# Twenty-four early gathers of a graph attention layer, put by in DRAM, and scores as columns of the first product

## The chip, the core and the metric

The kernel runs on one core of a Trainium2 chip. A core has TensorE (PE in the profile; its weight loads are listed apart as PEld), VectorE (DVE), ScalarE (ACT), GpSimd (POOL) and SyncE (SP, which here only issues DMAs), an on-chip memory of 128 partitions (SBUF), the accumulators of TensorE (PSUM), and 16 DMA engines to and from the chip's DRAM. Each engine runs its own instructions in order, and the engines wait for one another by semaphores. The metric is the time of one execution in microseconds on the device, the median of several runs.

## The reference

A layer norm (no scale or shift) and a ReLU, then a graph network with two attention layers (GAT), a two-layer perceptron, and the sum with the input. There are 6,250 nodes, 100,000 edges and one loop per node; inputs are float32, and the edges are sorted by destination.

```python
def gat_conv(x, src, dst, W, a_src, a_dst, bias, heads):
    h = (x @ W).reshape(n, heads, -1)
    alpha_s = (h * a_src[None]).sum(-1)
    alpha_d = (h * a_dst[None]).sum(-1)
    e = leaky_relu(alpha_s[src] + alpha_d[dst], 0.2)
    m = segment_max(e, dst);  e = exp(e - m[dst])
    alpha = e / (segment_sum(e, dst)[dst] + 1e-16)
    return segment_sum(h[src] * alpha[:, :, None], dst).reshape(n, -1) + bias

h = relu(layernorm(x))                     # 6250 x 768
h = relu(gat_conv(h, ..., W1, heads=4))    # 4 heads of 64
h = relu(gat_conv(h, ..., W2, heads=1))    # 1 head of 256
out = x + relu(h @ Wm1 + bm1) @ Wm2 + bm2
```

## The kernel before

The nodes are cut into NT = 49 tiles of 128, the edges into 782 tiles of 128 in their sorted order. Four edge tiles make a group (NG = 196 groups), four groups belong to a node tile.

**Stage 1** (lines 305 to 463) runs over the 49 node tiles. DVE takes means and variances (`moments`, L320 to L322) and subtracts the mean (`centre`, L339), ACT applies the ReLU (L341), and TensorE multiplies with W1 in six steps of K = 128 (`features1`, L350). A float32 product stands in the profile as two records, so a tile has twelve. ACT scales the result into a row tile `kept[i]` (`keep1`, L356). POOL multiplies it with the eight score vectors a_src, a_dst and adds it in halves (L365, L368); for the last four tiles DVE does this product (L375). DVE sums the rest (`scores1`, L377), ACT appends the four source scores to the row (L378), and `store1` (L381, SP) writes the row tile to `table[1]` in DRAM: 264 float32 per node, four heads of 64 and a one each, then four scores. `edge_places` loads and prepares the edge lists in small pieces, one per tile from tile 14 on; `first_places` (L278, at tile 40) makes the index lists of the early gathers.

**Layer 1** (`layer_edges` with `Node1`) and **layer 2** (`Node2`) then run over the 196 groups. `gather` (L545) has POOL fetch, for each edge tile, the 128 source rows out of `table` by one indirect DMA (L554), eight groups ahead of their use. Two edge tiles share a buffer; there are 2 * (AHEAD + 2) = 20 such pair buffers (L225). `meet` (L600) brings the destination's score to each edge by a product with a mask, `pair` (L612) makes the attention weights (ACT L619 and L621, DVE L624 and L634) and the weighted rows `hw` (DVE L636 in layer 1), and TensorE adds them up per destination with the one-hot matrix `hot` (DVE L582) into `o_ps` (L648). `gather_up` adds partial sums of groups, and `node.steps` (L796) finishes a node tile: it divides, turns it (two transposes into the PSUM tile `tp`), multiplies with the second layer's weights and writes the row to `table[2]` (L819). The steps are spread over the following groups by `rest(7)`: each `advance` (two per group) lets each pending node tile do one step, and near the end `rest` gives way at once. The PSUM tiles `tp` and `h_ps` take turns in two buffers (tag "n").

**Early gathers.** A gather from the whole table has to wait for the last row tile. `EARLY` lists gathers that read only the first `there` row tiles: sources beyond them are replaced by row 0 (`first_i`), multiplied with 0 (`first_ok`), and the missing rows added by a product of a one-hot matrix (`first_hits`, L258) with the row tiles that are still in SBUF (`first_whole`, L273 and L275). In layer 1 there are eight: four with `there` = NT - 5 and four with NT - 3, issued by POOL in stage 1's tiles NT - 4 and NT - 2 (`first_rows`, L300). Layer 2 has eleven.

The order on each engine is the program's order (`tc.manual_schedule()`, L304); a tile's buffer comes free when all its users are done. SP issues, in this order, what the loops ask for: x tiles, row stores, the destination rows `drow` (L521, three buffers), the masks (L573, kept in DRAM for layer 2), the rows of table 2.

Of the kernel before, what the change touches and what calls it, by code (L numbers as in the profile page):

```python
# [17 lines left out]
P = 128  # L18
# [28 lines left out]

EARLY = {1: ((4, NT - 5), (4, NT - 3)), 2: ((2, NT - 3), (9, NT - 2))}
THERE = {layer: [there for n, there in stages for _ in range(n)] for layer, stages in EARLY.items()}

@with_exitstack
def kernel(
# [52 lines left out]

    iota_ps = ps.tile([P, P], F32, name="iota_ps", bufs=1)
    nc.vector.tensor_copy(iota_ps, iota)
    eps_c = const.tile([P, 1], F32, name="eps_c")  # L110
    nc.vector.memset(eps_c, EPS)
# [77 lines left out]
    def edge_places(ones):  # L189

        dst_i = ones.tile([P, NET], I32, name="dst_i")
        dri = ones.tile([NCH, CH], I32, name="dri")
        for to, of in ((dst_i, dst_cols), (dri, dst_rows), (src_i, src_cols)):
            nc.sync.dma_start(to, of)
            yield
            yield
        for layer in bT:
# [64 lines left out]
    def first_whole(pool, layer):  # L262

        j = 0
        for stage, (n, there) in enumerate(EARLY[layer]):
            if stage and layer == 1:
                first_hits(pool, layer, stage)
            for k in range(n):
                pair, t = divmod(FIRST + j, 2)
                G = first_G[layer][pair][:, t]  # L270
                p = ps.tile([P, TW[layer]], F32, name="missing", tag="o", bufs=3)
                for T in range(there, NT):
                    nc.tensor.matmul(p, hits[stage, T][:, k * P:(k + 1) * P], kept[T][:, :TW[layer]],  # L273
                                     start=(T == there), stop=(T == NT - 1))
                nc.vector.scalar_tensor_tensor(G, G, first_ok[layer][:, j:j + 1], p, ALU.mult, ALU.add)  # L275
                j += 1
# [15 lines left out]
    def first_rows(layer, stage):  # L292
# [3 lines left out]
        for j in range(j, j + n):  # L296
            k, t = divmod(FIRST + j, 2)
            if k not in first_G[layer]:
                first_G[layer][k] = rows_in(layer)
            nc.gpsimd.indirect_dma_start(  # L300
                out=first_G[layer][k][:, t], out_offset=None, in_=table[layer][:there * P],
                in_offset=bass.IndirectOffsetOnAxis(ap=first_i[layer][:, j:j + 1], axis=0))
    mask_d = dram.tile([NU * P, 8 * P], BF16, name="mask_d")
    edges_stack.enter_context(tc.manual_schedule())  # L304
    with tc.tile_pool(name="w1p", bufs=1) as wp, tc.tile_pool(name="x1", bufs=6) as xp, \
# [38 lines left out]
        def features1(i):  # L344
            r, rstd = rs.pop(i)
            h_ps = ps.tile([P, HID], F32, name="h_ps", tag="o", bufs=3)
            for k in range(KI):
                if (i, k) == (1, 2):
                    spread_means(2)
                nc.tensor.matmul(h_ps, r[:, k], w1[:, k], start=(k == 0), stop=(k == KI - 1))  # L350
            return h_ps, rstd

        def keep1(i, h_ps, rstd):
            row = kept[i]
            h = heads_row(row)[:, :, :HID // 4]
            nc.scalar.activation(h, h_ps.rearrange("p (h c) -> p h c", h=4), AF.Copy, scale=rstd)  # L356

            ha = wk.tile([P, 8, HID // 4], F32, name="ha", bufs=2)
            four = ha.rearrange("p (k h) c -> p k h c", k=2)
            of = h.unsqueeze(1).to_broadcast([P, 2, 4, HID // 4])  # L360
            if i >= NT - 4:
                halves[i] = four, of
                return
            else:
                nc.gpsimd.tensor_tensor(four, of, a1b, ALU.mult)  # L365
                for n in (HID // 8, HID // 16):
                    hb = wk.tile([P, 8, n], F32, name=f"ha{n}", bufs=2 if n > 16 else 4)
                    nc.gpsimd.tensor_tensor(hb, ha[:, :, :n], ha[:, :, n:], ALU.add)  # L368
                    ha = hb
            halves[i] = ha  # L370

        def scores1(i):
            if i >= NT - 4:
                four, of = halves[i]
                nc.vector.tensor_tensor(four, of, a1b, ALU.mult)  # L375
                halves[i] = four.rearrange("p k h c -> p (k h) c")
            nc.vector.tensor_reduce(sd[1][:, i], halves.pop(i), AX.X, ALU.add)  # L377
# [18 lines left out]
        fetch_x(1)  # L396
        w1 = wp.tile([P, KI, HID], F32, name="w1")
        nc.sync.dma_start(w1, W1.rearrange("(k p) f -> p k f", p=P))
        fetch_xT(1)
# [5 lines left out]
        fetch_x(5)  # L405
        pieces = edge_places(ones)
        moments(0)
        spread_means(0)
# [5 lines left out]
        for i in range(NT):  # L414
# [23 lines left out]
            if i == 40:  # L438
                first_places()
            if i < NT - 5:  # L440
                keep1(i, *h)
                if i > 2:
                    store1(i - 3)
                if i > 1:
                    scores1(i - 2)
            else:
                for k in {NT - 3: (i - 2, i - 1)}.get(i, (i - 2,) if i < NT - 3 else (i - 1,)):
                    scores1(k)
                    if k == NT - 7:
                        store1(k - 1)  # L450
                    store1(k)
                keep1(i, *h)
            if i == NT - 6:
                first_sources(1)
            if i == NT - 4:
                first_rows(1, 0)
            elif i == NT - 2:
                first_rows(1, 1)
            if i >= 14:
                next(pieces, None)  # L460

        scores1(NT - 1)
        store1(NT - 1)

# [65 lines left out]
    def layer_edges(layer, H, node, pre, matched, pre_pool):  # L530
# [4 lines left out]
        with tc.tile_pool(name=f"eg{layer}", bufs=5) as eg, \  # L535
# [9 lines left out]
            def gather(g):  # L545
                if not 0 <= g < NG:
                    return
                for t in tiles(g):
                    k = TPG * g + t
                    if k // 2 not in G:  # L550
                        G[k // 2] = first_G[layer].get(k // 2) or rows_in(layer)
                    if k < FIRST + len(THERE[layer]):
                        continue
# [140 lines left out]
            if layer == 1:  # L694
                for r in range(4):
                    fetch_rows(r)
                first_whole(pre_pool, layer)
                for u in range(4):
# [9 lines left out]
            for g in range(NG):  # L708
# [14 lines left out]
                if j == 0:  # L723
                    if layer == 1:
                        fetch_rows(t + 4)
                    node.prefetch(t)
                    meet(t + 1)
                elif j == (2 if t < NT - 1 else 1):
                    node.ahead(t)
                elif j % 2:  # L730
                    make_mask((g + 7) // 2)
                if g == NG - 3:
# [40 lines left out]
    with tc.tile_pool(name="w2p", bufs=1) as wp, tc.tile_pool(name="wk2", bufs=2) as wk:  # L773
# [4 lines left out]
        class Node1:  # L778
# [17 lines left out]
            def steps(self, t, sum_, most=None, last=None):  # L796
# [12 lines left out]
                turn(o, p)  # L809
                yield from rest(7)  # L810
                rT = straighten(wk, 1, p)
                h_ps = ps.tile([P, HID + 2], F32, name="h_ps", tag="n")
                for k in range(KH):
                    nc.tensor.matmul(h_ps, rT[:, k], w2[:, k], start=(k == 0), stop=(k == KH - 1))
                yield from rest(7)
                row = kept[t][:, :TW[2]]
# [5 lines left out]
        with tc.tile_pool(name="pre1", bufs=1) as pre:  # L822
            first_hits(pre, 1, 0)
            pre1 = prepare(pre, 1, 4)
# [430 lines left out]
```

## Time and profile before

| | us |
|---|---|
| median of 3 runs | 2144.38 (2143.71 to 2145.70) |
| profiled execution | 2556.39 |
| its span, first to last instruction | 2554.4 |

The profiled execution is longer than the runs that were timed without the profiler, and every trace time below is on its clock.

| engine | busy us | share of the span | instructions |
|---|---|---|---|
| PE | 1572.4 | 62% | 6764 |
| DVE | 1325.8 | 52% | 4164 |
| ACT | 545.2 | 21% | 2601 |
| POOL | 1599.2 | 63% | 1759 |

Stage 1 takes the first 155 us, layer 1's edges reach to about 1355 us, layer 2's to the end. A group of the profile is read as: line, engine and operation, output <- inputs, shapes and count, then busy time in us and the mean of one in ns, then the idle time of its engine just before, with what ended most of it. Two rows as an example: the first product of stage 1, and the early completions' products.

```profile
L350 PE MATMUL h_ps<-w,r 128*128 128x256 f32 x588 | 135.0, 384 | 4.4 <-ACT r L341 4.4
L300 POOL DMA_INDIRECT G<-table,first_i x19 | 19.2, 1011 | 46.8 <-DVE e_ps L634 40.0 <-issue 4.9 <-DMA table<-kept 1.7
```

The records of L350 overlap: 588 of them have a mean of 384 ns, but only 135.0 us are busy. The L300 row is POOL's early gathers of both layers, 1.01 us each.

### The profile page before, as it was taken

The numbers are of one execution on the slowest core, as the hardware profiler recorded it, in microseconds if no ns is written. First come the engines' busy times: TensorE is split into PE (matmuls) and PEld (weight loads), VectorE is DVE, ScalarE is ACT, GpSimd is POOL, SyncE is SP. The second block draws the span as 40 slices with busy tenths as digits, with TensorE's granted clock in tenths as the row PEclk, the third lists the DMA queues.
The fourth block names the chain that finished last, engine by engine and source line by source line (L and its number), as shares of the span: only waits on it lengthen the run. The fifth ranks groups of instructions, "written<-read, shape, count | busy, mean of one in ns | idle before, by whom it ended". The sixth has DMA issues, their size and how long they took to land.

```text
span 2554.4 us, 26518 instructions
## 1 busy us (share of the span) xinstructions
PE 1572.4 (62%) x6764; PEld 1116.8 (44%) x6765; DVE 1325.8 (52%) x4164; ACT 545.2 (21%) x2601; POOL 1599.2 (63%) x1759
## 2 busy tenths in 40 slices
PE   9963455545554556546554557666676676666667
PEld 7852334433433334324342444444454444444444
DVE  7844555555655556546562444444444444444444
ACT  4630111111121111112121112222222222222212
POOL 6875666666666666666635566666666666666661
PEclk9986677667777777777776777777877787778789
DMA  9954454445454454444434444544554455445442
GB/s 353 344 164 145 128 148 138 132 138 150 135 147 140 136 149 141 137 136 146 138 91 134 125 134 130 152 149 136 155 151 144 142 153 152 144 144 153 147 150 66
DMA packets 157543, 383.12 MB, mean 150 GB/s; under 512 B 35543, under 2 KB 50222, under 8 KB 157382
## 3 DMA queue, kind: packets, MB, share of 16 engines
q0 software_dynamic: 75072, 209.10, 30.4%
q1 hardware_dynamic: 80940, 170.75, 19.1%
q10 hardware_dynamic: 1370, 1.48, 0.2%
q8 instruction: 58, 0.95, 0.1%
q14 instruction: 103, 0.84, 0.1%
HBM read 323.07 MB, written 58.13 MB: 149 GB/s over the span
## 4 chain that ended last, share of the span: by engine, by line
DVE 18%; another core or an unknown queue 15%; PE 14%; issue 13%; ACT 3%; DMA 0%; POOL 0%; ACTq 0%; DVEq 0%; POOLq 0%
PE o_ps L648 8%; DVE hw L631 6%; DVE hw L636 3%; PE y_ps L939 3%; DVE e_ps L624 2%; DVE w L627 1%; PE tp L923 1%; ACT sum L678 1%; DVE acc L669 1%; DVE y L942 1%; DVE e_ps L634 1%; PE e_ps L600 1%; DVE hot L582 1%; PE y_ps L875 0%
## 5 line engine op out<-in xcount | busy, mean ns | idle before, releaser
L554 POOL DMA_INDIRECT G<-table,src_i x1545 | 1469.0, 951 | 822.9 <-issue 535.8
L648 PE MATMUL o_ps<-hw,hot 128*128 128x260 f32 x1564 | 541.4, 482 | 316.2 <-issue 204.4
L648 PEld LDWEIGHTS o_ps<-hw,hot 128*128 128x128 f32 x1564 | 344.8, 235 | 482.5 <-issue 278.6
L648 PE MATMUL o_ps<-G,hw 128*128 128x258 f32 x1564 | 488.2, 460 | 61.3 <-issue 41.2
L648 PEld LDWEIGHTS o_ps<-G,hw 128*128 128x128 f32 x1564 | 352.8, 233 | 168.7 <-issue 59.6
L624 DVE TENSOR_TENSOR e_ps<-e,e_ps 128x8 f32<-128x8 f32 (+1 forms) x782 | 126.5, 162 | 515.7 <-ACT e L621 172.4
L678 ACT ACTIVATE sum<-acc 32x260 f32<-32x260 f32 (+1 forms) x384 | 159.9, 416 | 991.4 <-DVE acc L669 730.4
L600 PE MATMUL e_ps<-win,mask 128*128 128x12 bf16 (+1 forms) x1564 | 88.2, 169 | 372.7 <-issue 356.5
L636 DVE TENSOR_TENSOR hw<-G,e_ps 128x520 f32<-128x520 f32 x391 | 271.9, 695 | 76.9 <-DVE e_ps L634 46.3
L631 DVE TENSOR_SCALAR hw<-iota_ps,dcol,w 128x128 f32<-128x128 f32 x782 | 285.0, 406 | 17.7 <-DVE w L627 2.9
L600 PEld LDWEIGHTS <-mask 128*128 128x128 bf16 x1564 | 75.2, 103 | 393.5 <-issue 369.3
L942 DVE TENSOR_TENSOR y<-y_ps,xt 128x384 f32<-128x384 f32 (+1 forms) x98 | 54.0, 552 | 233.5 <-remote 209.6
L619 ACT ACTIVATE e<-G 128x8 f32<-128x8 f32 (+1 forms) x782 | 151.4, 195 | 110.5 <-issue 57.7
L939 PE MATMUL y_ps<-wm,mT 128*128 128x384 f32 x392 | 160.9, 535 | 11.1 <-issue 7.5
L582 DVE TENSOR_TENSOR hot<-iota_ps,dcol 128x512 f32<-128x512 f32 x196 | 133.5, 681 | 34.1 <-remote 34.1
L621 ACT ACTIVATE e<-G 128x8 f32<-128x8 f32 (+1 forms) x782 | 149.4, 192 | 0.0
L350 PE MATMUL h_ps<-w,r 128*128 128x256 f32 x588 | 135.0, 384 | 4.4 <-ACT r L341 4.4
L923 PE MATMUL tp<-rT,wm 128*128 128x128 f32 x392 | 68.0, 328 | 111.4 <-issue 81.9
L634 DVE TENSOR_TENSOR e_ps<-e_ps,e 128x8 f32<-128x8 f32 x391 | 68.1, 174 | 131.5 <-remote 96.4
L769 ACT ACTIVATE rT<-tp,bT 128x128 f32<-128x128 f32 x196 | 60.7, 362 | 293.5 <-remote 243.3
L350 PEld LDWEIGHTS h_ps<-w,r 128*128 128x128 f32 x588 | 109.7, 193 | 22.6 <-ACT r L341 5.7
L923 PEld LDWEIGHTS tp<-rT,wm 128*128 128x128 f32 x392 | 59.8, 229 | 125.6 <-issue 91.1
(405 smaller groups left out, 1201.3 us busy)
## 6 DMA issues: line engine op xcount, KB each, us to landing
xt<-in_x SPq DMA_DIRECT2D x96, 384.0 KB
drow<-dmod_d SPq DMA_DIRECT2D x49, 512.0 KB
mask_d<-mask SPq DMA_DIRECT2D x97, 256.0 KB
mask<-mask_d SPq DMA_DIRECT2D x97, 256.0 KB
G<-table,src_i POOLq DMA_INDIRECT x1545
xTt<-in_xT SPq DMA_DIRECT2D x49, 384.0 KB
out<-y SPq DMA_DIRECT2D x48, 384.0 KB
table<-kept SPq DMA_DIRECT2D x49, 132.0 KB
```

Of the source, the lines that this page charges most:

```text
L350: nc.tensor.matmul(h_ps, r[:, k], w1[:, k], start=(k == 0), stop=(k == KI - 1))
L554: nc.gpsimd.indirect_dma_start(out=G[k // 2][:, k % 2], out_offset=None, in_=table[layer], in_offset=bass.IndirectOffsetOnAxis(ap=src_i[:, ...
L582: nc.vector.tensor_tensor(hot[g][:, T[0]:T[0] + n], iota_ps.unsqueeze(1).to_broadcast([P, n, P]), dcol[:, k:k + n].unsqueeze(2).to_broadca ...
L600: nc.tensor.matmul(e_ps[t][:, at + k, :3 * H], m[:, k * P:(k + 1) * P], pre.win[:, 2 * u + 2], start=True, stop=True)
L619: nc.scalar.activation(e1, sc, AF.Exp)
L624: nc.vector.tensor_mul(v, e2, rho)
L631: nc.vector.tensor_scalar(hw[:, t], iota_ps, dcol[:, k:k + 1], w[:, t], ALU.is_equal, ALU.mult)
L636: nc.vector.tensor_mul(hw, Gp[:, :, :RW[1]].rearrange("p t (h c) -> p t h c", h=H), w.unsqueeze(3).to_broadcast([P, 2, H, C + 1]))
L648: nc.tensor.matmul(o_ps[u], l, r[:, :RW[layer]], start=(g % 2 == 0 and k == 0), stop=(g % 2 == 1 and k == tiles(g)[-1]))
L678: nc.scalar.activation(done[t][r], acc[r], AF.Copy)
L923: nc.tensor.matmul(m_ps[:, j], wm1[:, k, j * P:(j + 1) * P], rT[:, k], start=(k == 0), stop=(k == KH - 1))
L939: nc.tensor.matmul(y_ps, mT[:, j], wm2[:, j, s * half:(s + 1) * half], start=False, stop=(j == KH - 1))
```

## The change

**Early gathers of layer 1.** `EARLY[1]` goes. In its place twelve pairs of edge tiles (24 gathers) are listed in `SOON` by the number of row tiles that their gathers may read (NT - 11 to NT - 2); they belong to the pairs 23, 39, 55, ... 199, one in every eight groups (`SOON_AT`). In stage 1, from tile 35 on, each row tile is stored at once, and `soon_rows` issues the gathers that this row tile allows. When the edges begin, `soon_away` writes the twelve pair buffers to DRAM; `soon_back` reads one back where the loop before would have gathered it. `soon_sources`, `soon_hits`, `soon_missing` and `soon_whole` complete one edge tile per node tile for the first 24 node tiles: SP loads the source numbers, DVE makes the one-hot matrices in group 2 of the node tile, TensorE multiplies them with the row tiles in group 3 (into a PSUM tile of tag "n"), and DVE adds the product to the row in the next node tile's group 1. `rest(7)` becomes `rest(4)` in layer 1's steps.

**Scores.** W1 gets eight more columns, W1 times the score vectors, computed by POOL and DVE (`halve` and a reduce at tiles 2 to 4). From tile 8 (`BARE`) on the product has 264 columns, and ACT copies the scores from PSUM to the row and to `sd`. The first eight tiles still use POOL, at tiles 4 to 11, and DVE, at tiles 8 to 15. The index lists of the 24 gathers are made among the pieces of `edge_places`.

```diff
-EARLY = {1: ((4, NT - 5), (4, NT - 3)), 2: ((2, NT - 3), (9, NT - 2))}
+EARLY = {2: ((2, NT - 3), (9, NT - 2))}
+SOON = [NT - m for m in (11, 11, 10, 9, 8, 7, 6, 5, 4, 4, 3, 2)]
+SOON_AT = {2 * (8 * i + 11) + 1: i for i in range(len(SOON))}
+BARE = 8
...
+    def soon_places(i):
+        of = src_i[:, 2 * soon_pair[i]:2 * soon_pair[i] + 2]
+        nc.vector.tensor_scalar(soon_ok[:, i], of, float(SOON[i] * P), None, ALU.is_lt)
+        nc.vector.tensor_tensor(soon_i[:, i], of, soon_ok[:, i], ALU.mult)
+    def soon_rows(there):
+        for i in range(len(SOON)):
+            if SOON[i] == there:
+                soon_G[i] = rows_in(1)
+                for t in range(2):
+                    nc.gpsimd.indirect_dma_start(
+                        out=soon_G[i][:, t], out_offset=None, in_=table[1][:there * P],
+                        in_offset=bass.IndirectOffsetOnAxis(ap=soon_i[:, i, t:t + 1], axis=0))
+    def soon_away():
+        for i in range(len(SOON)):
+            nc.sync.dma_start(soon_d[i], soon_G.pop(i).rearrange("p t c -> p (t c)"))
+    def soon_back(i):
+        G = rows_in(1)
+        nc.sync.dma_start(G.rearrange("p t c -> p (t c)"), soon_d[i])
+        return G
+    def soon_sources(pool, i):
+        if i < len(SOON):
+            soon_of[i] = pool.tile([P, 2 * P], I32, name="soon_of", bufs=2)
+            nc.sync.dma_start(soon_of[i], bcast(src_rows, 2 * P, 2 * P * soon_pair[i]))
+    def soon_hits(pool, k):
+        i, t = divmod(k, 2)
+        if i < len(SOON):
+            m = NT - SOON[i]
+            soon_hit[k] = pool.tile([P, NT - SOON[0], P], F32, name="soon_hit")
+            nc.vector.tensor_tensor(
+                soon_hit[k][:, :m],
+                soon_of[i][:, t * P:(t + 1) * P].unsqueeze(1).to_broadcast([P, m, P]),
+                nid_ps[:, SOON[i]:].unsqueeze(2).to_broadcast([P, m, P]), ALU.is_equal)
+    def soon_missing(k):
+        if 0 <= k < 2 * len(SOON):
+            there, hit = SOON[k // 2], soon_hit.pop(k)
+            soon_p[k] = ps.tile([P, TW[1]], F32, name="missing1", tag="n")
+            for T in range(there, NT):
+                nc.tensor.matmul(soon_p[k], hit[:, T - there], kept[T], start=(T == there),
+                                 stop=(T == NT - 1))
+    def soon_whole(G, k):
+        if 0 <= k < 2 * len(SOON):
+            i, t = divmod(k, 2)
+            row = G[soon_pair[i]][:, t]
+            nc.vector.scalar_tensor_tensor(row, row, soon_ok[:, i, t:t + 1], soon_p.pop(k),
+                                           ALU.mult, ALU.add)
...
-            h_ps = ps.tile([P, HID], F32, name="h_ps", tag="o", bufs=3)
+            h_ps = ps.tile([P, HID + 8], F32, name="h_ps", tag="o", bufs=3)
+            n = HID if i < BARE else HID + 8
...
-                nc.tensor.matmul(h_ps, r[:, k], w1[:, k], start=(k == 0), stop=(k == KI - 1))
+                nc.tensor.matmul(h_ps[:, :n], r[:, k], w1[:, k, :n], start=(k == 0), stop=(k == KI - 1))
...
+            if i >= BARE:
+                nc.scalar.activation(row[:, RW[1]:], h_ps[:, HID:HID + 4], AF.Copy, scale=rstd)
+                nc.scalar.activation(sd[1][:, i], h_ps[:, HID:], AF.Copy, scale=rstd)
...
+        score_w = [halve(w1[:, k, :HID].rearrange("p (h c) -> p h c", h=4)) for k in range(KI)]
...
+            if 2 <= i < 2 + KI // 2:
+                for k in range(2 * i - 4, 2 * i - 2):
+                    nc.vector.tensor_reduce(w1[:, k, HID:], score_w[k], AX.X, ALU.add)
+            if BARE <= i < 2 * BARE:
+                scores1(i - BARE)
+            keep1(i, *h)
+            if 4 <= i < BARE + 4:
+                halves[i - 4] = halve(heads_row(kept[i - 4])[:, :, :HID // 4])
+            if BARE < i <= 2 * BARE:
+                store1(i - BARE - 1)
+            if BARE < i <= SOON[0] - 3:
+                store1(i - 1)
+            if i >= SOON[0] - 3:
+                store1(i)
+                soon_rows(i + 1)
...
             if layer == 1:
-                for r in range(4):
+                for r in range(3):
                     fetch_rows(r)
-                first_whole(pre_pool, layer)
+                soon_sources(pre_pool, 0)
+                soon_away()
+                fetch_rows(3)
                 for u in range(4):
                     make_mask(u)
...
-                yield from rest(7)
+                yield from rest(4)
```

## The prediction

> **What bounds the kernel now.** I read the groups of instructions first, for an engine whose work adds up to the time, then POOL alone in order of time, then the busy time by stretches. The largest group is the gather:
>
> ```profile
> L554 POOL DMA_INDIRECT G<-table,src_i x1545 | 1469.0, 951 | 822.9 <-issue 535.8
> L648 PE MATMUL o_ps<-hw,hot 128*128 128x260 f32 x1564 | 541.4, 482 | 316.2 <-issue 204.4
> L582 DVE TENSOR_TENSOR hot<-iota_ps,dcol 128x512 f32<-128x512 f32 x196 | 133.5, 681 | 34.1 <-remote 34.1
> ```
>
> POOL in order of time, where stage 1 ends and the edges begin:
>
> ```profile
> 143.32 1.26 POOL L368 TENSOR_TENSOR ha<-ha 128x256 f32<-128x256 f32 x2
> 146.25 1.13 POOL L300 DMA_INDIRECT G<-table,first_i  x1 [1.67 <-DMA table<-kept]
> ...
> 150.18 1.45 POOL L300 DMA_INDIRECT G<-table,first_i  x1 [0.30 <-issue]
> ...
> 154.52 1.30 POOL L300 DMA_INDIRECT G<-table,first_i  x1 [0.31 <-issue]
> 156.13 0.95 POOL L300 DMA_INDIRECT G<-table,first_i  x1 [0.30 <-issue]
> 157.48 0.97 POOL L554 DMA_INDIRECT G<-table,src_i  x1 [0.41 <-issue]
> 158.76 0.94 POOL L554 DMA_INDIRECT G<-table,src_i  x1 [0.30 <-issue]
> ```
>
> With nothing to wait for, a gather takes 0.95 us and 0.30 us pass before the next: 1.25 us. So of the 822.9 us of idle time, 1545 x 0.30 = 464 belong to the pace, 359 are real waits for consumers; one more wait of 40.0 us stands before layer 2's first early gather (1314 to 1354 us). The profiled execution took 2556.4 us (span 2554.4), the median is 2144.4: the 412 between them are nearly these 399. So the runs that are timed are the trace without POOL's waits: POOL gathers without a break. Check: early gathers start at 146.25, the last gather ends 52 us before the end of the span, 2 us lie outside it; 2144.4 - 2.0 - 146.3 - 52 = 1944 us for 1545 + 19 gathers, 1.243 us each with no gap at all, about 1.23 if 15 to 25 us of a gap stay between the layers. **I take 1.23 us per gather** (ends 1.22 and 1.25): the sum is made with POOL's own rows and subtracted from the median.
>
> Busy time by stretches (sum, instructions; then granted clock, DMA share, GB/s):
>
> ```profile
> 60.00:90.00 30.00, 30.00 (x146) 25.97 (x145) 26.69 (x69) 18.91 (x46) 26.66 (x34) 1.00 1.04 373
> ...
> 130.00:135.00 5.00, 3.47 (x9) 2.78 (x10) 4.10 (x12) 2.44 (x5) 2.37 (x3) 0.68 0.80 280
> ```
>
> Stage 1 is bound by PE: it is busy all of 60 to 90 us, a node tile takes 2.70 us; DVE and POOL (26.7 of 30 each) have little room. Over 300 to 1300 us (layer 1's edges, 669 gathers) the same view gives PE 535.5, DVE 563.9 us at a clock of 0.72: 0.80 and 0.84 us per edge tile, below 1.23.
>
> **Gathers.** Layer 1 has 782 edge tiles. Before, 8 are gathered early and 774 in the loop; after, 24 early and 758 in the loop. Sixteen fewer on the path: 16 x 1.23 = **-19.7 us**, if the 24 really lie beside stage 1. They replace POOL's score products there (1.18 + 1.26 us of each 2.70 from tile 12 on, now gone). Gathers begin when row 37 of 0..48 has landed; counted back from the last store T, with 2.78 us per tile (below) and 2.6 us from store to gather (scores of row 43 written at 143.6, gather at 146.25), that is T - 30.6 + 2.6; 24 x 1.25 = 30 us later is T + 2.0, and the last row lands at T + 2.6. So they fit, without a reserve.
>
> [...] The row: the eight early gathers take 8.71 us together, 1.09 each against 0.95, 1.45 and 1.30 beside DVE's `ha` product and `hit` compares. At 1.09 the 24 last 33.4 us and end at T + 5.4, 2.8 us late. [...] I take 0.95, and keep 2.8 us for the range.
>
> **Stage 1.** Products get 264 columns for 256 from tile 8 on: 2.59 us for twelve records (2.70 less 0.11 for the mean) x 8/256 = 0.081 per tile, x 41 = **+3.3 us** on the binding engine. Out go the DVE reduce (0.28) and ACT's copy; ACT gains one 0.2 us copy (stretch 60 to 90: 18.9 of 30, hidden by PE). Moving the pieces: six times two `soon_places`, four small DVE operations of 0.10 to 0.16 us, some 0.5 per tile into a slack of 0.36 + 0.28 + 0.08: nothing; uncovered it is 3 us. Score columns of w1: POOL needs 6 x 2.44 = 14.7 us from w1's arrival (before 11.3), so pairs are ready at 16.1, 21.0 and 25.9; DVE asks for them after the centring, near 21.6, 23.8 and 26.4: covered. If the write is ordered against products of the same buffer, up to 3 us; I take 0. A stall goes at tile 42:
>
> ```profile
> 126.89 1.18 POOL L365 TENSOR_TENSOR ha<-kept,a1b 128x512 f32<-128x512 f32 x1 [0.18 <-ACT kept L356]
> 126.92 1.17 DVE L284 TENSOR_SCALAR first_ok<-src_i 128x9 f32<-128x9 int32 x1
> ...
> 131.53 4.54 PE L350 MATMUL h_ps<-w,r 128*128 128x256 f32 x12 [2.42 <-ACT r L341]
> ```
>
> A compare of nine columns takes as long as POOL's product beside it, against 0.10 to 0.16 for its neighbours. The late centring costs PE 2.6 us, and the tile after it, at clock 0.68, another 1.8: 4.4. After the change four of the eight operations and POOL's products are gone; 0.5 us plus a memset of 0.7 stay, within a tile's slack: **-3.7 us** (ends -4.4 and 0). The tail: before, PE ends at 152.17 and the last store's data at 154.37, after two DVE products of 0.69. After, one ACT copy of 0.47 and one of 0.2 suffice: 1.5 us earlier. Sum for the last store: +3.3 - 3.7 - 1.5 = -1.9; its landing then gates the first edge gather. **I take -2 us** (ends -4 and +6[...]).
>
> **Stores and queues.** From tile 35 SP waits for the tile just computed before it fetches x again. x is six tiles ahead, and its last fetch is at tile 40, xT's at 43: covered, about 1 us if not. At the start of the edges twelve of the 20 pair buffers hold early rows. Eight pairs are free, 16 x 1.25 = 20 us of gathering. Ahead of the twelve 264 KB stores on SP stand two w2 loads and three `drow` rows, then one index row: some 2.1 MB, and 3.2 MB of stores. With the gathers' 95 GB/s (190 to 200 us) off the 350 to 410 of stage 1, an estimate of 230 GB/s: the first buffer is back after 10 us, all after 23, while the ninth is wanted at 20 and one each 2.5 us later. Covered. The fourth `drow`, which waits for masks, stands behind the stores. Each `soon_back` on SP waits for a buffer used ten groups earlier, long free; mask and row-2 stores behind it don't suffer. The 6.3 MB out and back over 950 us are 7 GB/s beside 139.
>
> **In the groups.** Twelve pairs miss 11, 11, 10, 9, 8, 7, 6, 5, 4, 4, 3, 2 table rows: 80 x 2 = 160 products. An edge product costs 541.4/782 = 0.69 us of busy PE at clock 0.72: 111 us. [...] Even by the dearer row: per node tile 16 x 0.80 + 11 x 0.69 = 20.4 us against POOL's 15 x 1.23 = 18.5; summed over tiles with 11, 10 and 9 missing rows the lag is 4 x 1.9 + 2 x 1.2 + 2 x 0.5 = 11 us, and gathers run 40 tiles, 49 us, ahead. DVE: `hot` is 1.33 ns per column, 160 x 128 columns 27 us, and 24 completions at 0.48 (the 128x264 form of L275) 12: 39 us in 24 node tiles, 13.4 + 1.9 + 0.5 = 15.8 of 18.5. Hidden by POOL. `first_whole` of layer 1 before the groups goes; POOL filled its buffers beside it, so I give it nothing, but up to 11 us (POOL's pause at 197 us) if that wait exists without the profiler. `rest(4)`: row 45 of table 2 is stored a group earlier, so two early gathers of layer 2 leave sooner: at most 2.5 us, **-1**.
>
> **Sum:** 2144.4 - 19.7 - 2 - 1 = 2121.7, **2122 us**.
>
> **Rivals.** (1) Stage 1 gives back: [...]+6 for -2: 2130. For it: no reserve in POOL's window; against: what disturbed is removed. 0.2. (2) The edges' start wait is real: 2122 - 11 = 2111; for it the pause at 197 us, against it that the median has no room for such waits. 0.08. (3) The parked buffers come back late: at a third of my estimated rate the twelfth is back after 69 us and wanted at 20 + 11 x 2.5 = 48, so POOL pauses 21 us: 2143, no change. 0.04. (4) Slower: PE becomes the bound in layer 1's first half. With clock c, a tile costs (9.2 + 0.5 m)/c, m missing rows; the lag passes the 49 us of lookahead below c = 0.62. At 0.55 it is 100 us, 51 more than covered: 2122 + 51 = 2173. For it: stretches of 0.60 in the trace; against: those are where PE idles (2.6 of 20 us at 220 to 240), dense ones have 0.8 to 1.0. 0.06. The first case keeps 0.62.
>
> **Range:** 2112 to 2134 holds the likeliest, rival 1 and a part of 2. A change under 0.2% (4.3 us) can't be told from none: faster 0.90, same 0.04, slower 0.06.
>
> **What would show it.** POOL: 24 gathers spaced 1.25 us ending within 1 us of the first edge gather, at 154 to 157 us; 758 + 771 in the loops; the gap of 0.30 on most of them. PE at tile 42 without a 4.5 us tile. The new products busy at a clock no lower than 0.7. Wrong would be: new long waits before layer 1's gathers named by PE or DVE, edge gathers starting after 160, a pause after the sixteenth.

## The result, and the profile after

The changed kernel takes 2122.80 us (median of 4, 2119.54 to 2125.66), the kernel before 2145.04 (2143.71 to 2146.03): a ratio of 0.989, 95% interval 0.988 to 0.991, so 22 us less, between 20 and 26. The forecast was 2122.

One thing has to be said of the profiles first. The two times of the result come from a chip on which the kernel before takes 2145 us, and the profile after has that speed too (2119.54 us). The profile of the kernel before that the prediction was made from took 2556.39 us. By that time it comes from another sort of chip: the experiments met chips on which the same kernel takes 2561 to 2577 us (medians of 10 to 23 executions, none under 2548). Times are compared below on one chip only, and positions in profiles on one sort, except where it is said. Of the kernel before there is no profile from the 2145 us sort.

The groups of the changed kernel that answer to those shown of before, and the two new ones:

```profile
L621 POOL DMA_INDIRECT G<-table,src_i x1529 | 1453.8, 951 | 466.2 <-issue 271.2
L331 POOL DMA_INDIRECT G<-table,soon_i x24 | 22.9, 952 | 86.7 <-DMA xt<-in_x 79.6
L715 PE MATMUL o_ps<-hw,hot 128*128 128x260 f32 x1564 | 544.5, 491 | 242.4 <-DVE hw L703 181.4
L366 PE MATMUL missing<-kept,soon_hit 128*128 128x264 f32 x320 | 91.6, 446 | 0.0
L424 PE MATMUL h_ps<-w,r 128*128 128x264 f32 (+1 forms) x588 | 136.1, 386 | 1.5 <-ACT r L414 1.4
```

POOL's 466 us of idle time before 1529 gathers are 0.305 us for each. Nothing is left for waits: on this chip POOL gathers without a break, as the prediction had concluded from the median. POOL in order of time, from the first of the 24 early gathers to the first edge gathers, then the boundary of the layers:

```profile
125.90 1.13 POOL L331 DMA_INDIRECT G<-table,soon_i  x1 [79.65 <-DMA xt<-in_x]
...
154.82 0.95 POOL L331 DMA_INDIRECT G<-table,soon_i  x1 [0.30 <-issue]
156.07 0.95 POOL L621 DMA_INDIRECT G<-table,src_i  x1 [0.30 <-issue]
...
1110.70 0.95 POOL L309 DMA_INDIRECT G<-table,first_i  x1 [0.30 <-issue]
...
1115.58 0.94 POOL L309 DMA_INDIRECT G<-table,first_i  x1 [2.62 <-DVE e_ps L701]
...
1127.64 0.94 POOL L621 DMA_INDIRECT G<-table,src_i  x1 [0.73 <-DMA wm<-in_Wm]
...
2091.35 0.95 POOL L621 DMA_INDIRECT G<-table,src_i  x1 [0.30 <-issue]
```

The whole time can be read off these starts. Layer 1 takes 1110.70 - 156.07 = 954.6 us for 758 gathers, 1.259 each; the boundary has eleven early gathers and one wait of 2.6 us; layer 2 has 771 gathers at 1.251; after the last one 25.5 us remain of the span of 2117.8. If a gather has the same price in the kernel before, sixteen fewer are 16 x 1.259 = **20.1 us** of the 22.

The stretches that were shown of before, with the same columns:

```profile
60.00:90.00 30.00, 30.00 (x142) 25.25 (x141) 25.59 (x78) 19.32 (x56) 0.00 (x0) 1.00 1.03 370
130.00:135.00 5.00, 4.93 (x23) 3.92 (x22) 4.11 (x11) 3.51 (x11) 3.78 (x5) 1.00 1.04 338
```

PE is still the bound of stage 1, with a little fewer records in 30 us (142 for 146: the tile has grown), and POOL, 26.7 us busy there before, does nothing. From 130 to 135 us PE, busy 3.47 of 5 us before at a clock of 0.68, is now busy throughout. The rows at that place, on DVE and on PE:

```profile
127.11 0.17 DVE L293 TENSOR_SCALAR first_ok<-src_i 128x9 f32<-128x9 int32 x1
```

```profile
127.56 2.84 PE L424 MATMUL h_ps<-w,r 128*128 128x264 f32 x12
...
130.57 2.94 PE L424 MATMUL h_ps<-w,r 128*128 128x264 f32 x12
```

The compare of nine columns takes 0.17 us with no product of POOL beside it, where it took 1.17, and PE no longer waits 2.4 us before that tile.

### The profile page after: what moved, and what is told of

The parts are those of the page before. It is cut to its first block, busy times and chain, and to the rows that moved or that the text cites. A ratio compares the mean times of both kernels' runs of the same rounds, so it can differ in the third digit from the quotient of the medians.

```text
span 2117.8 us, 27038 instructions
## 1 busy us (share of the span) xinstructions
PE 1611.4 (76%) x7019; PEld 1124.3 (53%) x7021; DVE 1354.6 (64%) x4178; ACT 598.2 (28%) x2642; POOL 1524.8 (72%) x1666
## 4 chain that ended last, share of the span: by engine, by line
DMA 30%; PE 25%; DVE 22%; issue 11%; POOL 5%; ACT 5%; ACTq 0%; DVEq 0%; POOLq 0%; SPq 0%
DMA G<-table,src_i 30%; PE o_ps L715 10%; DVE hw L703 7%; PE h_ps L424 6%; POOL G L621 5%; PE y_ps L1015 5%; DVE e_ps L691 2%; DVE hw L698 2%; DVE e_ps L701 2%; ACT sum L745 2%; ACT e L686 2%; DVE mask L638 2%; DVE acc L736 1%; ACT e L688 1%; PE tp L999 1%
## 5 line engine op out<-in xcount | busy, mean ns | idle before, releaser
L621 POOL DMA_INDIRECT G<-table,src_i x1529 | 1453.8, 951 | 466.2 <-issue 271.2
L715 PE MATMUL o_ps<-hw,hot 128*128 128x260 f32 x1564 | 544.5, 491 | 242.4 <-DVE hw L703 181.4
L715 PE MATMUL o_ps<-G,hw 128*128 128x258 f32 x1564 | 466.5, 434 | 234.0 <-DVE hw L698 233.3
L715 PEld LDWEIGHTS o_ps<-G,hw 128*128 128x128 f32 x1564 | 313.4, 213 | 358.7 <-DVE hw L698 298.6
L1015 PE MATMUL y_ps<-wm,mT 128*128 128x384 f32 x392 | 201.5, 649 | 0.7 <-ACT mT L1004 0.7
L424 PE MATMUL h_ps<-w,r 128*128 128x264 f32 (+1 forms) x588 | 136.1, 386 | 1.5 <-ACT r L414 1.4
L1015 PEld LDWEIGHTS y_ps<-wm,mT 128*128 128x128 f32 x392 | 86.8, 245 | 66.6 <-issue 38.2
L366 PE MATMUL missing<-kept,soon_hit 128*128 128x264 f32 x320 | 91.6, 446 | 0.0
L736 DVE SCALAR_TENSOR_TENSOR acc<-acc,keep,o_ps 128x260 f32<-128x260 f32 (+1 forms) x192 | 91.1, 474 | 0.0
L331 POOL DMA_INDIRECT G<-table,soon_i x24 | 22.9, 952 | 86.7 <-DMA xt<-in_x 79.6
L366 PEld LDWEIGHTS missing<-kept,soon_hit 128*128 128x128 f32 x320 | 75.3, 235 | 17.9
L694 DVE TENSOR_TENSOR w<-e_ps,e 128x2 f32<-128x2 f32 x391 | 62.1, 159 | 13.3
```

The source lines that it names most:

```text
L366: nc.tensor.matmul(soon_p[k], hit[:, T - there], kept[T], start=(T == there), stop=(T == NT - 1))
L424: nc.tensor.matmul(h_ps[:, :n], r[:, k], w1[:, k, :n], start=(k == 0), stop=(k == KI - 1))
L621: nc.gpsimd.indirect_dma_start(out=G[k // 2][:, k % 2], out_offset=None, in_=table[layer], in_offset=bass.IndirectOffsetOnAxis(ap=src_i[:, ...
L715: nc.tensor.matmul(o_ps[u], l, r[:, :RW[layer]], start=(g % 2 == 0 and k == 0), stop=(g % 2 == 1 and k == tiles(g)[-1]))
L1015: nc.tensor.matmul(y_ps, mT[:, j], wm2[:, j, s * half:(s + 1) * half], start=False, stop=(j == KH - 1))
```

## Experiments

The theory: the time is the number of gathers in the loops times some 1.25 us, from where stage 1 lets the first begin; the consumers' new work lies beside it. The rivals: the new products make TensorE the bound, or the early gathers and score columns act by stage 1 rather than by the gathers' number. Each kernel was timed against the kernel before on its own chip. The chips on which the kernel before takes 2561 to 2577 us are called the 2570 us sort below, the others the 2145 us sort.

**More work for the consumers, and fewer gathers.** Two kernels on a chip where before takes 2149.85 us. The products twice:

```diff
-            for T in range(there, NT):
-                nc.tensor.matmul(soon_p[k], hit[:, T - there], kept[T], start=(T == there),
-                                 stop=(T == NT - 1))
+            for _ in range(2):
+                for T in range(there, NT):
+                    nc.tensor.matmul(soon_p[k], hit[:, T - there], kept[T], start=(T == there),
+                                     stop=(T == NT - 1))
```

> The 160 products of the early gathers are issued twice over in each group (the second pass writes the same rows of the pair's bank), so TensorE has some 91 us more work in the loops by the row of after (160 instructions' records of 0.446 us x 2). On a chip where the kernel before takes about 2145 us: if POOL's gathers are the bound and TensorE's work lies beside them, as the prediction has it, the time stays within 5 us of 2123; if TensorE is at the edge of being the bound (the fourth rival), layer 1 lengthens by 30 us and more, to 2150 or above, and POOL shows long waits that end with PE or DVE. On a chip where it takes about 2560 to 2577 us: the first run of this kernel stood 27 us above the one beside it; 50 us above the kernel before again if the work of the consumers is what counts there.

Eighteen pairs (the buffers of the first ones put away during stage 1, since there are 20 in all):

```diff
-SOON = [NT - m for m in (11, 11, 10, 9, 8, 7, 6, 5, 4, 4, 3, 2)]
+SOON = [NT - m for m in (18, 17, 16, 15, 14, 13, 12, 11, 11, 10, 9, 8, 7, 6, 5, 4, 3, 2)]
...
+                if i >= 41:
+                    soon_away(i - 4)
```

> 18 pairs of early gathers instead of 12: 12 gathers fewer in the loops. On a chip where the kernel before takes about 2145 us: if the time is the number of gathers in the loops times their spacing of 1.25 us, it falls by 15 us from 2123, less up to 3 us for early gathers that are still running when stage 1 ends, so 2108 to 2112; if the longer products of these groups (up to 18 tiles of rows in one pair) make the gathers wait, 2123 or above with waits of POOL in the first 500 us. On a chip where the kernel before takes about 2560 us: the first run gave 1.016 of it, and the same again is expected.

Measured: the products twice 2125.61 us, ratio 0.9885 (0.9868 to 0.9901); eighteen pairs **2117.01 us, ratio 0.9845 (0.9829 to 0.9862)**, a gain, but short of the 2108 to 2112 expected. The first is no slower against its before than the change itself (0.9893). Its groups, and then the busy time from 300 to 600 us, the changed kernel's first and its own below:

```profile
L622 POOL DMA_INDIRECT G<-table,src_i x1529 | 1457.5, 953 | 466.4 <-issue 274.0 <-ACT e L689 46.9 <-PE o_ps L716 40.5
L716 PE MATMUL o_ps<-hw,hot 128*128 128x260 f32 x1564 | 516.0, 473 | 213.7 <-DVE hw L704 165.4 <-DVE kept L896 46.0
L367 PE MATMUL missing<-kept,soon_hit 128*128 128x264 f32 x640 | 155.0, 402 | 0.0
```

```profile
300.00:600.00 300.00, 232.36 (x1048) 174.25 (x1047) 235.93 (x639) 73.66 (x382) 227.18 (x240) 0.85 0.65 182
```

```profile
300.00:600.00 300.00, 258.21 (x1281) 205.98 (x1279) 239.87 (x651) 68.82 (x396) 227.65 (x238) 0.93 0.63 183
```

PE is busy 258 of 300 us and POOL's idle time stays at 0.305 us a gather: TensorE's work was hidden with room for as much again. The fourth rival falls on this sort of chip. The granted clock is higher, 0.93 for 0.85: 320 more records add 63 us to their own group, but PE's total grows by only 35 (1611.4 to 1646.5), since the products beside them take less (`o_ps` by `hot` 516.0 us for 544.5).

Eighteen pairs against twelve with their products doubled, one chip: 8.6 us less by the medians. Its POOL in order of time, and a row of DVE, say how that comes about:

```profile
105.12 1.13 POOL L331 DMA_INDIRECT G<-table,soon_i  x1 [58.62 <-DVE rstd L405]
...
149.54 0.94 POOL L331 DMA_INDIRECT G<-table,soon_i  x1 [4.53 <-DVE cent L413]
...
161.75 0.94 POOL L331 DMA_INDIRECT G<-table,soon_i  x1 [0.30 <-issue]
163.00 0.94 POOL L624 DMA_INDIRECT G<-table,src_i  x1 [0.30 <-issue]
```

```profile
148.31 0.95 DVE L413 TENSOR_TENSOR cent<-xTt,mean_ps 128x768 f32<-128x768 f32 x1 [6.39 <-DMA xTt<-in_xT]
```

The first edge gather stands at 163.0 for 156.05, 6.9 us late. From it to the first early gather of layer 2 twelve gathers fewer save 956.6 - 942.8 = 13.9 us. The sum, -6.9, agrees with the 7.0 us by which the last gather is earlier (2087.95 for 2094.94). So each part of the theory is seen with its size: the gathers' number, and the start. The opposite test, as many gathers as before with the new stage 1, was run on the other sort only. The late start is, by the order on SP, this kernel's own doing: its stores of the parked buffers stand on SP ahead of the last loads of xT (seven of them take SP 6.65 us from 134.94 on), so the centring waits 6.4 us and the rows come late. This version beats both kernels, though by less than twelve gathers are worth. Putting the buffers away later, or a number of pairs between, was not tried.

**The 2570 us sort of chip.** All other runs came to three chips of this sort. First the kernel before once more, and the changed one:

> The kernel before, profiled once more, to see whether its long waits belong to it. Theory (POOL's gathers set the time): 2145 us; in an undisturbed profile POOL has no waits beyond the 0.30 us between gathers, 774 gathers of layer 1 take 774 x 1.26 = 975 us from about 157 us on, and the pause of 10.8 us at 197 us is gone. Rival (the start of the edges): the pause of about 10 us after the 40th gather stands in an undisturbed profile too, and the changed kernel's gain comes half from it.

> The kernel before, once more, for a profile on the kind of chip of the timed runs. Where it takes about 2145 us: 774 + 771 edge gathers at 1.25 us from 157.4 us on, no long waits of POOL, and a spacing that says what 16 gathers are worth (1.25: 20 us). If the time there is instead made of waits for the groups' work, gaps of several us stand ahead of some of its gathers, as in the profile that the prediction was made from.

> The changed kernel once more, beside the kernel before on the same chip. Theory (where POOL's gathers set the time, 16 x 1.255 us go): where the kernel before takes 2145 us, 2122.8 us; where it takes 2576 us and its consumers, not POOL, set the time, the 16 gathers buy nothing and the added products (PE and DVE work in layer 1) cost 10 to 40 us: 2585 to 2615 us. Rival (the gathers count everywhere): 20 us less than before on either chip.

Measured: before again 2577.04 (0.9997, 0.9982 to 1.0012) and 2574.93 (1.0007, 0.9984 to 1.0029); after again 2572.37 for 2561.12, **1.0042 (1.0028 to 1.0056)**. So here the change costs 11 us. All 10 to 20 executions of each kernel are long here, and on the 2145 us sort a profiled execution is as short as the others: the long waits of the profile of before are no effect of profiling. They stay with the change, here in the profile of after on this sort:

```profile
L621 POOL DMA_INDIRECT G<-table,src_i x1529 | 1455.1, 952 | 851.3 <-issue 581.7 <-ACT mT L1004 123.3 <-ACT e L688 70.0
L715 PE MATMUL o_ps<-hw,hot 128*128 128x260 f32 x1564 | 555.9, 486 | 385.7 <-issue 280.5 <-DVE hw L703 50.3 <-DVE e_ps L701 17.0
```

```profile
393.65 0.59 PE L715 MATMUL o_ps<-hw,hot 128*128 128x260 f32 x1 [1.51 <-issue]
...
395.06 0.59 PE L715 MATMUL o_ps<-hw,hot 128*128 128x260 f32 x1 [0.81 <-issue]
...
396.48 4.11 PE L715 MATMUL o_ps<-hw,hot 128*128 128x260 f32 x8 [0.83 <-issue]
...
397.27 0.39 ACT L894 ACTIVATE kept<-h_ps 128x257 f32<-128x257 f32 x1 [7.21 <-remote]
...
399.79 0.94 POOL L621 DMA_INDIRECT G<-table,src_i  x1 [4.93 <-issue]
```

The operations shown take the same time each (the gather 952 ns for 951, DVE's `hot` 682 for 680), but PE sends single products with pauses of 0.8 to 1.5 us here, ACT and DVE go on only after them, and POOL pauses: 130 of its 1529 gathers wait longer than the usual 0.3 us, half of them 3.5 us or more. That the pauses have no releaser says little, since these profiles hold few releasers at all: 12966 semaphore events are recorded for 42984 in the profile of the result, with 27039 instructions for 27038. ACT's waits for gathers, first in the profile of the result and then in this one:

```profile
ACT e L686 <- DMA G<-table,src_i: 955.0, 505, 5.4
```

```profile
ACT e L686 <- DMA G<-table,src_i: 13.5, 6, 2.7
```

A wait for a DMA or for another engine would look the same in this profile. Where POOL waits for the groups' work, fewer gathers should earn nothing and more work in the groups can cost. Three kernels on one chip (before: 2576.39 us) test that: the products twice, as above; each pair reading one row tile less, with 184 products for 160 (the first added line, "one tile sooner"); four pairs in place of twelve (the second).

```diff
-SOON = [NT - m for m in (11, 11, 10, 9, 8, 7, 6, 5, 4, 4, 3, 2)]
+SOON = [NT - m for m in (12, 12, 11, 10, 9, 8, 7, 6, 5, 5, 4, 3)]
+SOON = [NT - m for m in (5, 4, 3, 2)]
```

> Every completing product is computed twice (the second set overwrites the first): 160 more products, 91 us more busy PE in layer 1's first half. Theory (hidden behind POOL's gathers): 2122.8 us within 2, POOL's gaps stay 0.30. Rival (PE is at the edge of being the bound there): PE's 16 x 0.73 + 22 x 0.57 = 24.2 us per node tile against POOL's 18.8, long waits of POOL named by PE or DVE, +20 to +60 us.

> The changed kernel with every pair's missing rows one more (12, 12, 11, ... 3), so that POOL may begin one node tile sooner. Theory (the twenty-four gathers started 3 us late, because a row took 5.9 us to land beside the loads of x, and POOL then ran to 155.8 us while the last row had landed near 153.5): first edge gather near 153.5 us instead of 156.1, time -2.5: 2120.3 us. Rival (the last row's landing or the start of SP's loads sets it): first edge gather unchanged, 2122.8 us.

> The changed kernel with four pairs (5, 4, 3, 2 rows missing) instead of twelve: 8 early gathers as before, score columns and everything else as after. Theory: 16 gathers more in the loop at 1.255 us are +20.1 us, and the edges can begin at the last row's landing, near 153.5 us instead of 156.1, -2.5: 2140.4 us. Rival (the gain came from the lighter start of the edges and the columns): no change, 2123 us within 3.

Measured: products twice 2629.22 (1.0226, 1.0184 to 1.0268), one tile sooner 2601.67 (1.0119, 1.0082 to 1.0155), four pairs 2598.83 (1.0109, 1.0069 to 1.0150). The first fits: with 136 products more than one tile sooner it stands 28 us above it, while on the 2145 us sort 160 more cost nothing. The second gained nothing: its early gathers begin hardly sooner, at 125.70 us for 126.38 in the profile of after on this sort. The third does not fit: with as many gathers as before and 28 products for 160 it should have stood near before, and it stands 22 us above. On another chip:

> 4 pairs of early gathers, not 12: 774 gathers in the loop of layer 1, as many as before, and 28 products instead of 160, with the score columns kept. Where the kernel before takes about 2145 us: if the gathers' number is what the change earns by, all but some 3 us of the gain goes (the last store's landing then lets the edge gathers begin at about 154.5 us instead of 157.4): 2140 to 2143, a ratio of about 0.9985. If the new stage 1 earns by itself, or if the groups with fewer products go faster, the ratio stays at 0.995 or below.

2595.67 for 2573.87 (1.0087, 1.0062 to 1.0111), again 22 us above. Eighteen pairs, against a before of 2562.07 us:

> Eighteen pairs (36 early gathers, the first ones missing 18 row tiles), put away from tile 41 on instead of all at the start of the edges; 12 gathers fewer in the loop than the changed kernel, 81 x 2 products more. Theory, where the kernel before takes about 2145 us (POOL's gathers set the time): 12 x 1.255 = 15 us less than the changed kernel, and the gathers no longer start late, 0 to 2.5 us more: 2105 to 2109 us, ratio to before 0.982. Where it takes about 2570 us (consumers set the time): no gain, 1.005 to 1.02 of before. Rival (a price for early gathers that grows with their number: put-away traffic, PE): no gain over the changed kernel's 0.989 on the first kind of chip either.

2593.48 for 2562.07 (1.0157, 1.0105 to 1.0208). So twelve pairs cost 11 us, four 22 and eighteen 31, each against its own before: no order by gathers or by products.

Two places of the loss can be read from the profiles. The first is late in layer 1. From the 501st of its 782 gathers to the last, the kernel before takes 418 to 422 us in three profiles of this sort, and the kernels with four or twelve pairs take 436 to 444 in seven. By then the last early edge tile is long complete (at 826 us at the latest, and the 501st gather begins at 894 or later), so of the change only `rest(4)` is still at work in these groups. That would explain why four pairs are no better than twelve; `rest(4)` was not run alone on either sort, so it is argued and not shown. On the 2145 us sort the same 281 gathers take 353 us, their own pace.

The second is the end of stage 1, where the two sorts part as well. With twelve pairs the edges begin at 166.86, 164.70 and 167.36 us on the 2570 us sort (after, one tile sooner, products twice), for 156.07 and 156.05 on the other. In the first of them POOL's early gathers pause for 5.69 us, two centrings of DVE wait 5.17 and 5.67 us, and the last row lands late:

```profile
160.68 0.94 POOL L331 DMA_INDIRECT G<-table,soon_i  x1 [0.30 <-issue]
166.86 0.94 POOL L621 DMA_INDIRECT G<-table,src_i  x1 [5.24 <-DMA table<-kept]
```

That is 9 to 11 us after the starts of before on that sort (155.63 to 157.48). What holds the centrings up is not recorded. Four pairs show none of this. They leave POOL idle, so the last row's landing opens the edges: at 154.47 us on the chip where before's first edge gather stands at 157.38, at 155.25 where it stands at 155.63:

```profile
154.47 0.96 POOL L621 DMA_INDIRECT G<-table,src_i  x1 [3.19 <-DMA table<-kept]
```

The starts of before differ by one row, PE's tile after the stall of 2.42 us: 4.54 us in the profile of the prediction, 2.86 in the one that starts at 155.63, whose row follows. In the profile with the start at 157.38 the later tiles stand where they stand in that of the prediction (141.40 for 141.42 us).

```profile
131.41 2.86 PE L350 MATMUL h_ps<-w,r 128*128 128x256 f32 x12 [2.42 <-ACT r L341]
```

**The score columns.** The 24 early gathers without them: W1 with 256 columns, POOL's products per tile (DVE's in the last thirteen), DVE's reduce. The rows are then stored, and their gathers issued, one tile later.

```diff
-            n = HID if i < BARE else HID + 8
+            n = HID
...
-            if i >= BARE:
-                nc.scalar.activation(row[:, RW[1]:], h_ps[:, HID:HID + 4], AF.Copy, scale=rstd)
-                nc.scalar.activation(sd[1][:, i], h_ps[:, HID:], AF.Copy, scale=rstd)
+            of = heads_row(row)[:, :, :HID // 4]
+            if i >= NT - 13:
+                ha = wk.tile([P, 8, HID // 4], F32, name="ha", bufs=2)
+                halves[i] = ha, of
+            else:
+                halves[i] = halve(of)
...
+                soon_rows(i)
```

> The twelve pairs without the score columns: products of 256 columns, POOL's score products up to tile 35, DVE's (0.69 + 0.69 us, as before for the last four tiles) from tile 36 on. Theory, where the kernel before takes about 2145 us: the columns pay by freeing POOL and DVE in the last tiles; without them a tile costs DVE 3.66 us for 2.70, some 9 us over the tiles up to 45, the stall at tile 42 stays and each early gather runs at 1.1 us beside DVE's products, so that the edges begin 8 to 14 us later than 156 us: 2131 to 2137 us, 0.995 of before. Rival (the columns only cost PE 3.3 us and the early gathers alone bring the gain): 2119 to 2123 us, 0.988. Where the kernel before takes about 2570 us: 1.005 to 1.01 of before by either.

> The 24 early gathers are kept, but the scores of stage 1 are made as before (two products on VectorE or GpSimd and a reduction for each tile, in the old order of steps), with the rows that go to DRAM stored one tile later. Where the kernel before takes about 2145 us: if the score columns are what lets the early gathers run beside stage 1 without lengthening it, the first edge gather begins about 8 us later than with them (164.9 us in this kernel's first run) and the time is 2130 to 2132, a ratio of about 0.993; if they add nothing, 0.989 as with them.

Measured 2570.84 for 2562.07 (1.0036, 1.0024 to 1.0049) and 2588.68 for 2573.87 (1.0053, 1.0034 to 1.0072). With the columns the same sort gave 1.0042, so there the columns make no difference that shows. That can't be carried to the 2145 us sort. PE at the end of stage 1 in the second run:

```profile
143.42 2.86 PE L424 MATMUL h_ps<-w,r 128*128 128x256 f32 x12 [0.41 <-ACT r L414]
...
146.80 2.86 PE L424 MATMUL h_ps<-w,r 128*128 128x256 f32 x12 [0.41 <-ACT r L414]
```

PE waits for ACT at almost every tile: one takes 3.37 us in the last thirteen, for 2.78 with the columns, 13 x 0.59 = 7.7 us. The edge gathers begin at 164.85 and 170.69, but with the columns they begin at 164.70 to 167.36 on this sort, so an earlier start by the columns is not seen here. About 8 us of the start on the 2145 us sort is an estimate from the tile's length alone; no run measured it.

## Why the prediction held, step by step

**The bound.** Right: POOL gathers without a break. The reason given for it was half wrong. The 412 us between the profiled execution and the others were put down to waits that the profiled execution alone has; they are waits of another sort of chip, and stand in all its executions. In part it was luck that the step held: the median that the gain was subtracted from came from the chip of the result. On the 2570 us sort the same change is 11 us slower.

**Price of a gather.** 1.23 us was taken within 1.22 to 1.25; it is 1.259 in layer 1, just outside. The spacing was worked out with a tail of 52 us from that other profile; it is 25.5 us, and 26.5 us over 1564 gathers are 0.017 each, which makes its 1.243 into 1.260. The 15 to 25 us of gap between the layers, taken off to come to 1.23, are a single wait of 2.6. POOL's own rows, 0.95 + 0.30, came closer. The gathers gave 20.1 us for the 19.7 forecast.

**The 24 early gathers.** They lie beside stage 1, spaced 1.25 us, and the edge gathers follow without a gap, as foretold. Their start was mis-sized: 2.6 us from the store of row 37 to the first gather. SP issues the store at 120.00 and POOL begins at 125.90, 5.9 us, where the DMA share is 1.01 (120 to 126 us); the 2.6 were read where it is 0.10 (143 to 147 us of before). So they end at 155.77, 5.0 us after the last store is issued and not 2.0, and become what opens the edges, at 156.07 us. Four pairs, with the landing of the last row to open them, begin at 154.47 and 155.25 (on the 2570 us sort): an estimate of 0.8 to 1.6 us given away. Longer early gathers, for which the prediction kept 2.8 us, do not show in the changed kernel: 22.9 us for 24 are 0.95 each, beside DVE's `stats` and `cent`. Of before's eight, the one that begins 0.06 us after an `ha` product of DVE (150.18 after 150.12) took 1.45 us, the one that begins beside its `hit` compares (154.52, compares from 154.04 on) 1.30, and the one that begins 0.48 us after an `ha` product (153.19 after 152.71) 1.03. In the two profiles without the columns, where DVE makes these products in the last thirteen tiles, four early gathers took 1.28 to 1.41. What makes them longer is not shown by these profiles.

**Stage 1.** The tile is 2.78 us, the stall at tile 42 is gone, the columns of W1 and the index pieces cost nothing that shows. For the last store -1.9 us was forecast; it is issued at 150.8, and the early gathers hide what it gains. Across the two sorts, the start of the edges moved from 157.48 to 156.07, -1.4 for -2; against a before whose tile after the stall is not slow (155.63) it would be +0.4. Of the stall's -3.7 us only the 2.4 of the wait are there each time.

**Stores and queues.** Right in effect: no pause after the sixteenth gather.

**In the groups.** Right for the chip of the result: 160 products took 91.6 us, 0.57 each, between the row's 0.69 and 0.445, an estimate from stage 1 of before (twelve records in 2.59 us at a granted clock of 1.00, with 264 columns for 256). Doubled they take 0.48 each, at a mean granted clock of 0.93 for 0.85 from 300 to 600 us: the denser work came nearer to stage 1's price. It does not carry over to the 2570 us sort, where doubling the products costs (2629.22 us for 2576.39) and the change alone makes the total 0.4% longer. The fourth rival described such a case, but by a low clock; what is seen is pauses (granted 0.76 to 0.78 there from 270 to 570 us, with PE busy 208 of 300).

**Rest.** The gathers give 20.1 of the 22.2 us. The other 2.1, with the result uncertain by 3 either way, are the start, `rest(4)` and the missing `first_whole` together, forecast at 2, 1 and 0. Without a profile of before from the 2145 us sort they can't be told apart. A further gain of 11 us from the edges' start (the second rival) has no room there. The third rival falls by the missing pause, the first by the start at 156.07.

## What to carry to other kernels

Where one engine works without a break, a change is priced by that engine's own rows: the number of its instructions times its spacing, and the moment it can start; the other engines' added work can be doubled as a test of whether it is hidden. When a profile and the timed runs differ by much, find out whether they come from the same chip before a cause is given, since what earns on the one sort can cost on the other. Before a pause is called one without a cause, see how many releasers the profile holds. And a side job has to be kept out of the queue that feeds the main one: with seven stores ahead of one load of xT, six more pairs lost 6.9 us at the start of the 13.9 that they gained.

## What the runs showed of the hardware

- Chips differ by 20% on one program: 2145 and 2150 us in the result and in one set of the runs, 2561 to 2577 on three other chips, with the same duration of the operations compared (gather 951 and 952 ns) and the difference in pauses, whose cause the profiles don't record.
- With 160 products more on TensorE, the mean granted clock from 300 to 600 us was 0.93 for 0.85, and the neighbours took less: `o_ps` by `hot` 516.0 us for 544.5.
- An indirect gather takes 0.95 us on POOL (1529 in 1453.8 us). In the kernel before, one that began 0.06 us after a 128x512 product of DVE took 1.45, one that began 0.22 us before such a product 0.95.
- A nine-column compare on DVE took 1.17 us beside POOL's 128x512 product (before), 0.17 where POOL made none (after).
- After one stall of 2.42 us the same PE tile took 4.54 us in one profile of the kernel before and 2.86 in another.
